# A four-layer graph network kernel: rows of the bf16 pieces of layers one and three padded from 391 to 400 columns

## The chip, the cores and the metric

The kernel runs on one core of one Trainium2 chip. Its time is the device time of one execution in microseconds (us). Lower is better. Three runs of the kernel before gave 3,763.98, 3,763.66 and 3,755.65 us; their median is 3,763.66 us.

## The reference

The input is `x` (3,327 nodes × 512 values, float32) and `adj` (3,327 × 3,327, zero or one). Four layers follow each other. Each first normalises the rows of `x` and takes the positive part (`h`), and adds its result to `x`. Layers one to three are graph attention with 8, 4 and 8 heads, the fourth is an average over neighbours between two dense products:

```python
h = relu(layernorm(x))
Wh = h @ W                                     # per head: 64 columns (128 in the second layer)
e = leaky_relu(f1[:, None] + f2[None, :], 0.2) # f1 = Wh.a1, f2 = Wh.a2, one number a node and head
e = where(adj > 0, e, -9e15)                   # second layer: adj with self loops
x = x + elu(softmax(e, axis=-1) @ Wh)
...
agg = (adj > 0) @ h / max(deg, 1)              # fourth layer
x = x + relu(concat(h @ W_self + b_self, agg @ W_nb + b_nb) @ W_comb + b_comb)
```

## The kernel before, in words

**The algebra.** A leaky ReLU has two slopes, and exp(f1 + f2) is a product. So the weight of neighbour j for node i is one of two products, and which one depends only on the sign of f1(i) + f2(j). The kernel therefore prepares two versions of each node's row: A, scaled by exp(f2), and B, scaled by exp(0.2 f2). Each version has DA = 65 columns a head in layers one and three: 64 of `Wh` and one with the scale itself, whose sum is the softmax's denominator. Each is split into three bf16 pieces, so that their sum has nearly float32's precision: 3 · 65 = 195 columns. For each pair of nodes, a 0-or-2 weight in fp8 says whether A counts (`tht`) or B (`gt`), and attention is then `tht.T @ A + gt.T @ B`.

**Names.** `dims(l)` (L102 to L107) gives the heads H, DA, AO (the column at which B begins in a row: 196 = 195 + one column of ones) and HW (the row's length). In layers one and three (`l` = 0 and 2) the row has 2 · 196 − 1 = 391 columns, A's 195, the one column of ones at 195 that A and B share, and B's 195 from column 196. `abd` (L109 to L116) are these rows in DRAM, a tensor for each group of node tiles. The second layer (`l` = 1) has other rows: A and B apart, 388 columns of bf16 each (L112, L580), or 258 of float32 (L577).

**Tiles.** There are 26 tiles of 128 nodes (the last has 127). As neighbours they go in five groups `JG` of 6, 6, 6, 4 and 4 tiles, as queries in chunks of four (the last has two). `jj` is a tile's place in its group; I call it the row within the group. A tile `ab` holds a group's rows side by side, 6 · 391 columns a partition, row `jj` from column 391 · `jj`.

**A head of a chunk** (`attention`, L505). SP's queue loads `s1b` (L518) and the five groups of `ab` (`load_pieces`, L498 to L503; seven buffers). For each neighbour tile ScalarE (L549) or, for some tiles, VectorE (L546) compares f1 with −f2 into `gt`; two VectorE operations on a whole group combine this with the mask into `tht` and `gt` (L555, L556; seven buffers each). TensorE then runs over the 26 neighbour tiles for two query tiles at a time: for each of the two it loads `tht` as weights and multiplies A's columns (L584), and loads `gt` and multiplies B's (L587), both into one PSUM bank `acc`, A at column 0, B at column AO. So the order is A, B for one query tile, A, B for the next, then the next neighbour tile. In head 0 of layer one alone (`deg`) both products take one column more, the ones, at column 195 (`o` = 1: A ends with it, B begins with it): its sum is the node's degree, copied out by L605. After each pair VectorE adds the three pieces up out of PSUM (L602).

**Work in between.** After each pair `hooks.run` (L471) issues a step of other work: transposing a part of the mask (L187 to L211, layer one), finishing a node tile of this layer (L647) and normalising and projecting it for the next (L397 to L422). That projection writes the pieces: `pieces` (L298) writes ones by a POOL memset (L308), copies two of the pieces by ScalarE (L317, L321), subtracts the third by POOL (L319), and SP stores the tile `pt` to `abd` (L327). For layer one this runs ahead of the attention, in its own stage with two node tiles a store; for layer three it runs inside layer two.

**Order and placement.** The instructions of an engine run in the order that the framework's scheduler gave them from the program's order and from edges that the code adds (`after`, L141). SP's queue issues its DMAs in that order too. Pools of layer `l` lie where an earlier pool lay, and a tile waits for the tiles that lay in its place; `lay_out` (L663) fixes the places, with a `gap` of 20 KB in layer one (L709) that moves `gt` past the stage before it.

Of the kernel before, what the change touches and what calls it, by code (L numbers as in the profile page):

```python
# [25 lines left out]
F32 = mybir.dt.float32  # L26
BF16 = mybir.dt.bfloat16
I32 = mybir.dt.int32
U32 = mybir.dt.uint32
FP8 = mybir.dt.float8e4  # L30
F32R = mybir.dt.float32r
AF = mybir.ActivationFunctionType
ALU = mybir.AluOpType
# [4 lines left out]
P = 128  # L38
# [14 lines left out]
def tile_gnn(ctx: ExitStack, tc: tile.TileContext, x, adj, W0, a01, W1, al, ar, W2, a2,  # L53
# [47 lines left out]

    def dims(l):  # L102

        H = heads[l]
        DA = D // H + 1
        AO = 3 * DA + 1
        return H, DA, AO, (2 * AO - 1 if l != 1 else 2 * AO)  # L107

    abd = []  # L109
    for l in range(3):  # L110
# [187 lines left out]
    def pieces(L, t, AB, pool, first):  # L298

        l = L.l  # L300
        g, jj = jwhere[t]
        H, DA, AO, HW = dims(l)

        o, two = (t % 2, 2) if first else (0, 1)
        if o == 0:
            L.pt = pool.tile([P, H, 2, two, AO] if l == 1 else [P, H, two, HW], BF16, name="pt", bufs=3 if first else 2)
        pt = L.pt
        nc.gpsimd.memset(pt[:, :, :, o, 3 * DA:AO] if l == 1 else pt[:, :, o, 3 * DA:AO], 1.0)  # L308

        def dst(s, a):  # L310
            if l == 1:
                return pt[:, :, a, o, s * DA:(s + 1) * DA]
            return pt[:, :, o, a * AO + s * DA:a * AO + (s + 1) * DA]
        r = pool.tile([P, 2, H, DA], F32, name="r", bufs=2 if first else 1)
        nc.vector.tensor_sub(r, AB, high(AB))  # L315
        for a in range(2):
            nc.scalar.copy(dst(0, a), high(AB[:, a]))  # L317
        for a in range(2):
            nc.gpsimd.tensor_sub(dst(2, a), r[:, a], high(r[:, a]))  # L319
        for a in range(2):  # L320
            nc.scalar.copy(dst(1, a), high(r[:, a]))  # L321
        js = slice(jj + 1 - two, jj + 1)
        if o == two - 1 and l == 1:
            for a in range(2):
                nc.sync.dma_start(abd[l][g][:, a, :, js, :].rearrange("h p j w -> p h j w"), pt[:, :, a])
        elif o == two - 1:
            stored[t] = nc.sync.dma_start(abd[l][g][:, :, js, :].rearrange("h p j w -> p h j w"), pt).ins.name  # L327
# [170 lines left out]
    def load_pieces(L, pool, g, h):  # L498

        nj = JG[g][1]  # L500
        tl = pool.tile([P, JM * 391], BF16, name="ab", bufs=7)
        v = tl[:, :nj * 391].rearrange("p (j w) -> p j w", j=nj)
        return v, nc.sync.dma_start(v, abd[L.l][g][h])  # L503

    def attention(L, hooks, open_next, close):  # L505
# [5 lines left out]
        for c, (t0, nt) in enumerate(chunks):  # L511
# [4 lines left out]
            for h in range(H):  # L516
# [44 lines left out]
                for a in range(2 if l == 1 else 1):  # L561
# [5 lines left out]
                    for ks, js in passes:  # L567
                        thr = {}
                        for j in js:
                            g, jj = jwhere[j]  # L570
                            if l == 1 and KIND[g] != "b" and g not in thr:
                                thr[g] = real(a, g, ks, th)
                            for k in ks:
                                if j == 0:
                                    acc[k] = accs.tile([P, 512], F32, name="acc")
                                if g in thr:
                                    mm = nc.tensor.matmul(acc[k][:, :2 * DA], thr[g][:, k - ks[0], jj, :], ab[a][g][:, jj, :],  # L577
                                                     start=(j == 0), stop=(j == NT - 1), skip_group_check=True)
                                elif l == 1:
                                    mm = nc.tensor.matmul(acc[k][:, :3 * DA], th[a][g][:, k, jj, :], ab[a][g][:, jj, :3 * DA],  # L580
                                                     start=(j == 0), stop=(j == NT - 1), skip_group_check=True)
                                else:
                                    o = 1 if deg else 0
                                    nc.tensor.matmul(acc[k][:, :3 * DA + o], th[0][g][:, k, jj, :],  # L584
                                                     ab[0][g][:, jj, :3 * DA + o], start=(j == 0), stop=False,
                                                     skip_group_check=True)
                                    mm = nc.tensor.matmul(acc[k][:, AO - o:HW], th[1][g][:, k, jj, :],  # L587
                                                     ab[0][g][:, jj, AO - o:HW], start=False, stop=(j == NT - 1),
                                                     skip_group_check=True)
                            if j == JG[3][0]:  # L590
                                late = mm.ins.name
                        if l == 2 and last and h == H - 1:
                            load_y2(yp, 0, late)
                        if js[-1] != NT - 1:
                            continue
                        for k in ks:
                            if l == 1:
                                nc.vector.tensor_reduce(R[:, k, a, :], acc[k][:, :3 * DA].rearrange("p (s d) -> p d s", s=3),
                                                        AX.X, ALU.add)
                            else:  # L600
                                v = acc[k][:, :2 * AO].rearrange("p (a w) -> p a w", a=2)[:, :, :3 * DA]
                                nc.vector.tensor_reduce(R[:, k], v.rearrange("p a (s d) -> p a d s", s=3), AX.X, ALU.add)  # L602
                            if deg:
                                n = pn(t0 + k)
                                nc.vector.tensor_copy(deg2[:n, t0 + k:t0 + k + 1], acc[k][:n, 3 * DA:AO])  # L605
                        gone.append(mm.ins.name)
                        hooks.run(1 if last else 3, hook, 2 if hook % 2 and c == 0 or hook % 3 == 0 and c else 1)
                        hook += 1
# [54 lines left out]
    def lay_out(pool, *tags):  # L663
        for name, n, dt, bufs in tags:
            pool.tile([P, n], dt, name=name, bufs=bufs)
# [8 lines left out]
    lay_out(rp, ("s1b", WMAX, F32, 2))  # L674
    masking = ExitStack()
    bp = masking.enter_context(tc.tile_pool(name="pieces", bufs=1))
    lay_out(bp, ("ab", JM * 391, BF16, 7))
    ip = masking.enter_context(tc.tile_pool(name="masks", bufs=1))
    with tc.tile_pool(name="first", bufs=1) as fp:


        lay_out(fp, ("pt", 16 * 391, BF16, 3), ("AB", 1040, F32, 2), ("r", 1040, F32, 2), ("hT", D, F32, 2))
        xa = []

        def first_x(t, lead=6):
# [15 lines left out]
        while hooks.tiles or hooks.flying:  # L701
# [3 lines left out]
                    ahead[g] = load_pieces(L, bp, g, 0)  # L705
            n += 1
    A, R = ("A", D, F32, 6), ("R", PER * 2 * 129, F32, 1)
    ab, gt, tht = ("ab", JM * 391, BF16, 7), ("gt", PER * JM * P, FP8, 7), ("tht", PER * JM * P, FP8, 7)
    tags = [[A, R, tht, ("gap", 20 * 1024, FP8, 1), gt],  # L709
            [("A", D, F32, 5), ("ab", JM * 258, F32R, 7), R, ("t6", 2 * JM * P, F32R, 4), tht[:3] + (6,), gt[:3] + (6,)],  # L710
            [A, ab, R, tht, gt]]
    hooks.masks = [lambda t=t, g=g: load_mask(ip, t, g) for t in range(NT) for g in range(len(JG))][hooks.done:]
# [532 lines left out]
```

## Time and profile before

| | |
|---|---|
| median of the runs | 3,763.66 us (3,755.65 to 3,763.98) |
| the profiled execution, its own time | 3,765.72 us |
| its span, first to last instruction | 3,763.9 us |
| mean granted TensorE clock | 0.976 of full |
| TensorE busy | 3,548.0 us (94%) |
| VectorE, ScalarE, POOL busy | 2,641.0 (70%), 2,519.9 (67%), 565.1 us (15%) |
| stage before layer one's attention | 0 to about 178 us |
| attention of layer one (L584, L587) | 178 to 1,269 us |
| layer two (L577, L580) | 1,286 to 2,250 us |
| attention of layer three (L584, L587) | 2,279 to 3,404 us |
| fourth layer (L781) | 3,436 to 3,748 us |
| DMA | 773 MB, mean 205 GB/s |
| `ab` loads of layers one and three | 336 of 586.5 KB, 224 of 391.0 KB |
| `pt` stores of layers one and three | 13 of 1,564 KB, 26 of 782 KB |

In the profile PE is TensorE's matmuls, PEld its weight loads, DVE is VectorE, ACT ScalarE, POOL GpSimd, SP the engine whose queue issues most DMAs. Ln is line n of the kernel. Matmuls overlap in the pipe, so their durations add up to more than the time that passed; the distance from one start to the next tells the pace. A wait is put down to what ended it last, and idle time of an engine that others don't wait for costs nothing.

### The profile page before, as it was taken

What the parts mean: (1) busy time and instruction counts of PE and PEld (TensorE: products, weight loads), DVE (VectorE), ACT (ScalarE), POOL (GpSimd) and SP (SyncE); (2) the same over time, 40 slices, a digit from 0 to 9 for tenths busy, and PEclk for the clock granted to TensorE, in tenths of its full rate; (3) what the DMA queues carried; (4) which work ended last, traced back from release to release, by engine and by line L of the source; (5) the groups of instructions that cost most, each with busy time, mean ns of one, the idle gap of its engine ahead of it and who ended that gap; (6) DMA issues with size and microseconds to landing.
All of it is one profiled execution on the core that took longest, in us unless ns stands there. A gap on an engine that the chain in (4) does not pass through costs nothing. (4 is left out here: it accounts for less than half of the span.)

```text
span 3763.9 us, 78861 instructions
## 1 busy us (share of the span) xinstructions
PE 3548.0 (94%) x31348; PEld 3198.3 (85%) x31348; DVE 2641.0 (70%) x5230; ACT 2519.9 (67%) x4170; POOL 565.1 (15%) x832
## 2 busy tenths in 40 slices
PE   7799999999999888999999978999999999999998
PEld 5699999999999677887887867999898989886886
DVE  7688888888777677878778766776766767672221
ACT  5677887778788667777768766776766767572111
POOL 6502221202101101122122121010000101010000
PEclk9899999999999999999999999999999999999999
DMA  7777767777657767767767786555555545576431
GB/s 216 225 207 212 218 203 220 224 219 223 206 191 247 247 226 246 237 220 251 251 215 243 250 282 200 185 180 163 188 169 167 192 159 194 163 259 237 129 102 50
DMA packets 321403, 773.06 MB, mean 205 GB/s; under 512 B 36037, under 2 KB 143560, under 8 KB 320384
## 3 DMA queue, kind: packets, MB, share of 16 engines
q1 hardware_dynamic: 293920, 707.23, 57.6%
q0 software_dynamic: 27104, 60.69, 6.6%
q8 instruction: 249, 4.08, 0.4%
q14 instruction: 130, 1.06, 0.1%
HBM read 661.25 MB, written 128.68 MB: 210 GB/s over the span
## 5 line engine op out<-in xcount | busy, mean ns | idle before, releaser
L549 ACT ACTIVATE gt<-s1b,ks 128x512 fp8e4<-128x512 f32 (+1 forms) x2968 | 1759.9, 678 | 291.1 <-issue 150.4
L584 PE MATMUL acc<-ab,tht 128*128 128x195 bf16 (+1 forms) x10816 | 1875.6, 248 | 20.5 <-DVE tht L555 15.0
L587 PE MATMUL acc<-ab,gt 128*128 128x195 bf16 (+1 forms) x10816 | 1874.9, 249 | 3.9 <-DVE gt L556 3.1
L584 PEld LDWEIGHTS <-tht 128*128 128x128 fp8e4 x10816 | 1061.0, 98 | 27.2 <-DVE tht L555 16.1
L587 PEld LDWEIGHTS <-gt 128*128 128x128 fp8e4 x10816 | 1053.7, 97 | 28.3 <-issue 16.1
L555 DVE TENSOR_TENSOR tht<-gt,m 128x768 uint32<-128x768 uint32 (+3 forms) x700 | 557.5, 798 | 184.7 <-ACT gt L549 179.7
L577 PE MATMUL acc<-ab,t 128*128 128x258 f32 x4160 | 576.4, 298 | 72.8 <-DVE t L493 62.5
L577 PEld LDWEIGHTS acc<-ab,t 128*128 128x128 f32 x4160 | 543.9, 200 | 100.8 <-DVE t L493 76.6
L556 DVE TENSOR_TENSOR gt<-tht,m 128x768 uint32<-128x768 uint32 (+3 forms) x700 | 563.4, 806 | 8.5
L546 DVE TENSOR_SCALAR gt<-s1b,ns 128x512 fp8e4<-128x512 f32 (+1 forms) x672 | 318.3, 485 | 142.0 <-PE acc L587 140.0
L781 PE MATMUL acc<-y,mf 128*128 128x512 f32 x1352 | 309.8, 391 | 1.3 <-DVE mf L776 1.3
L657 POOL TENSOR_TENSOR xt<-xt,e 128x512 f32<-128x512 f32 x78 | 113.1, 1450 | 1273.3 <-DVE e L656 1228.6
L781 PEld LDWEIGHTS acc<-y,mf 128*128 128x128 f32 x1352 | 253.5, 188 | 57.4 <-DVE mf L776 1.8
L602 DVE TENSOR_REDUCE R<-acc 128x130 f32<-128x390 f32 x416 | 214.8, 556 | 82.9 <-PE acc L587 82.8
L778 ACT CAST mf<-m 128x768 fp32r<-128x768 fp8e4 (+1 forms) x78 | 59.1, 762 | 244.7 <-PE acc L781 232.9
L493 ACT CAST t<-gt 128x1536 fp32r<-128x1536 fp8e4 x104 | 150.6, 1473 | 101.8 <-PE acc L577 101.6
L340 PE MATMUL mm<-w,hT 128*128 128x260 f32 (+1 forms) x832 | 200.2, 393 | 17.3 <-ACT hT L138 11.4
L319 POOL TENSOR_TENSOR pt<-r 128x520 bf16<-128x520 f32 (+1 forms) x116 | 139.2, 1219 | 369.2 <-DVE r L315 304.2
L340 PEld LDWEIGHTS mm<-w,hT 128*128 128x128 f32 x832 | 157.3, 194 | 42.4 <-ACT hT L138 14.0
L377 PE MATMUL mm<-w,hT 128*128 128x512 f32 x352 | 159.3, 596 | 0.0
L493 ACT CAST t<-tht 128x1536 fp32r<-128x1536 fp8e4 x104 | 149.7, 1462 | 9.0 <-DVE tht L555 5.7
L289 ACT ACTIVATE h<-xt,mv 128x512 f32<-128x512 f32 x104 | 84.2, 811 | 101.9 <-POOL mv L287 101.9
(132 smaller groups left out, 2893.1 us busy)
## 6 DMA issues: line engine op xcount, KB each, us to landing
ab<-ab SPq DMA_DIRECT2D x336, 586.5 KB
ab<-ab SPq DMA_DIRECT2D x224, 391.0 KB
ab<-ab SPq DMA_DIRECT2D x112, 774.0 KB
ab<-ab SPq DMA_DIRECT2D x112, 516.0 KB
ab<-ab SPq DMA_DIRECT2D x56, 582.0 KB
s1b<-s SPq DMA_DIRECT2D x120, 256.0 KB
m<-mask SPq DMA_DIRECT2D x72, 384.0 KB
ab<-pt SPq DMA_DIRECT2D x40, 516.0 KB
```

What stands on the lines that cost most here:

```text
L340: nc.tensor.matmul(pw, hT[:, k, :], L.w[:, k, f, :], start=(k == 0), stop=(k == KC - 1))
L377: nc.tensor.matmul(pw, hT[:, k, :], L.w[i][:, k, :], start=(k == 0), stop=(k == KC - 1))
L493: (nc.scalar.copy if KIND[g] == "s" else nc.vector.tensor_copy)(t[:, :k1 - k0, :nj], th[a][g][:, k0:k1])
L546: nc.vector.tensor_scalar(gv[:, :, jj, :], s1v, L.ns2[:, j, h:h + 1], 2.0, op0=ALU.is_gt, op1=ALU.mult, saturate=False)
L549: nc.scalar.activation(gv[:, :, jj, :], s1v, AF.Relu, bias=L.ks2[:, j, h:h + 1], scale=BIG, saturate=False)
L555: nc.vector.tensor_tensor(pu, gu, mu, ALU.bitwise_and)
L556: nc.vector.tensor_tensor(gu, pu, mu, ALU.bitwise_xor)
L577: mm = nc.tensor.matmul(acc[k][:, :2 * DA], thr[g][:, k - ks[0], jj, :], ab[a][g][:, jj, :], start=(j == 0), stop=(j == NT - 1), skip_grou ...
L584: nc.tensor.matmul(acc[k][:, :3 * DA + o], th[0][g][:, k, jj, :], ab[0][g][:, jj, :3 * DA + o], start=(j == 0), stop=False, skip_group_che ...
L587: mm = nc.tensor.matmul(acc[k][:, AO - o:HW], th[1][g][:, k, jj, :], ab[0][g][:, jj, AO - o:HW], start=False, stop=(j == NT - 1), skip_gro ...
L602: nc.vector.tensor_reduce(R[:, k], v.rearrange("p a (s d) -> p a d s", s=3), AX.X, ALU.add)
L781: nc.tensor.matmul(acc[k], mf[:, jj, :], y2[g][:, jj, s, :], start=(j0 + jj == 0 and s == 0), stop=(j0 + jj == NT - 1 and s == 1))
```

## The change

Rows of layers one and three get 400 columns in place of 391, 800 bytes in place of 782. AO, the column at which B begins, becomes 200, so B begins 400 bytes after A and each row 800 bytes after the one before. A and B now have a column of ones each, at 195 and 395, and four more columns that no product reads (196 to 199, 396 to 399). The memset fills five columns of both halves. The matmuls take the same number of columns as before: 195, or 196 in head 0 of layer one; B's go to columns 200 and up of `acc`. The degree is now the sum of two columns of `acc`, 195 and 395. Tiles, DRAM tensors, loads and stores grow with the row, and the gap in layer one's placement shrinks from 20 to 19 KB. The second and fourth layers compute as before.

```diff
@@ -101,10 +101,11 @@
 
     def dims(l):
 
+
         H = heads[l]
         DA = D // H + 1
-        AO = 3 * DA + 1
-        return H, DA, AO, (2 * AO - 1 if l != 1 else 2 * AO)
+        AO = -(-(3 * DA + 1) // 8) * 8 if l != 1 else 3 * DA + 1
+        return H, DA, AO, 2 * AO
 
     abd = []
     for l in range(3):
@@ -305,7 +306,8 @@
         if o == 0:
             L.pt = pool.tile([P, H, 2, two, AO] if l == 1 else [P, H, two, HW], BF16, name="pt", bufs=3 if first else 2)
         pt = L.pt
-        nc.gpsimd.memset(pt[:, :, :, o, 3 * DA:AO] if l == 1 else pt[:, :, o, 3 * DA:AO], 1.0)
+        nc.gpsimd.memset(pt[:, :, :, o, 3 * DA:AO] if l == 1 else
+                         pt[:, :, o].rearrange("p h (a w) -> p h a w", a=2)[..., 3 * DA:AO], 1.0)
 
         def dst(s, a):
             if l == 1:
@@ -498,8 +500,9 @@
     def load_pieces(L, pool, g, h):
 
         nj = JG[g][1]
-        tl = pool.tile([P, JM * 391], BF16, name="ab", bufs=7)
-        v = tl[:, :nj * 391].rearrange("p (j w) -> p j w", j=nj)
+        HW = dims(L.l)[3]
+        tl = pool.tile([P, JM * HW], BF16, name="ab", bufs=7)
+        v = tl[:, :nj * HW].rearrange("p (j w) -> p j w", j=nj)
         return v, nc.sync.dma_start(v, abd[L.l][g][h])
 
     def attention(L, hooks, open_next, close):
@@ -584,8 +587,8 @@
                                     nc.tensor.matmul(acc[k][:, :3 * DA + o], th[0][g][:, k, jj, :],
                                                      ab[0][g][:, jj, :3 * DA + o], start=(j == 0), stop=False,
                                                      skip_group_check=True)
-                                    mm = nc.tensor.matmul(acc[k][:, AO - o:HW], th[1][g][:, k, jj, :],
-                                                     ab[0][g][:, jj, AO - o:HW], start=False, stop=(j == NT - 1),
+                                    mm = nc.tensor.matmul(acc[k][:, AO:AO + 3 * DA + o], th[1][g][:, k, jj, :],
+                                                     ab[0][g][:, jj, AO:AO + 3 * DA + o], start=False, stop=(j == NT - 1),
                                                      skip_group_check=True)
                             if j == JG[3][0]:
                                 late = mm.ins.name
@@ -602,7 +605,8 @@
                                 nc.vector.tensor_reduce(R[:, k], v.rearrange("p a (s d) -> p a d s", s=3), AX.X, ALU.add)
                             if deg:
                                 n = pn(t0 + k)
-                                nc.vector.tensor_copy(deg2[:n, t0 + k:t0 + k + 1], acc[k][:n, 3 * DA:AO])
+                                nc.vector.tensor_reduce(deg2[:n, t0 + k:t0 + k + 1],
+                                                        acc[k][:n, 3 * DA:AO + 3 * DA + 1:AO], AX.X, ALU.add)
                         gone.append(mm.ins.name)
                         hooks.run(1 if last else 3, hook, 2 if hook % 2 and c == 0 or hook % 3 == 0 and c else 1)
                         hook += 1
@@ -674,12 +678,12 @@
     lay_out(rp, ("s1b", WMAX, F32, 2))
     masking = ExitStack()
     bp = masking.enter_context(tc.tile_pool(name="pieces", bufs=1))
-    lay_out(bp, ("ab", JM * 391, BF16, 7))
+    lay_out(bp, ("ab", JM * 400, BF16, 7))
     ip = masking.enter_context(tc.tile_pool(name="masks", bufs=1))
     with tc.tile_pool(name="first", bufs=1) as fp:
 
 
-        lay_out(fp, ("pt", 16 * 391, BF16, 3), ("AB", 1040, F32, 2), ("r", 1040, F32, 2), ("hT", D, F32, 2))
+        lay_out(fp, ("pt", 16 * 400, BF16, 3), ("AB", 1040, F32, 2), ("r", 1040, F32, 2), ("hT", D, F32, 2))
         xa = []
 
         def first_x(t, lead=6):
@@ -705,8 +709,8 @@
                     ahead[g] = load_pieces(L, bp, g, 0)
             n += 1
     A, R = ("A", D, F32, 6), ("R", PER * 2 * 129, F32, 1)
-    ab, gt, tht = ("ab", JM * 391, BF16, 7), ("gt", PER * JM * P, FP8, 7), ("tht", PER * JM * P, FP8, 7)
-    tags = [[A, R, tht, ("gap", 20 * 1024, FP8, 1), gt],
+    ab, gt, tht = ("ab", JM * 400, BF16, 7), ("gt", PER * JM * P, FP8, 7), ("tht", PER * JM * P, FP8, 7)
+    tags = [[A, R, tht, ("gap", 19 * 1024, FP8, 1), gt],
             [("A", D, F32, 5), ("ab", JM * 258, F32R, 7), R, ("t6", 2 * JM * P, F32R, 4), tht[:3] + (6,), gt[:3] + (6,)],
             [A, ab, R, tht, gt]]
     hooks.masks = [lambda t=t, g=g: load_mask(ip, t, g) for t in range(NT) for g in range(len(JG))][hooks.done:]
```

## The prediction

> **What bounds the kernel now.** I read the page's shares and slices first, then the cost groups, then a table of stretches, and last the timeline of the matrix engine inside one head. From the page (engine, busy us, share, instructions; then tenths of busy time in 40 slices; then line, engine, op, count | busy us, mean ns of one | idle before, releaser):
>
> ```profile
> span 3763.9 us, 78861 instructions
> PE 3548.0 (94%) x31348; PEld 3198.3 (85%) x31348; DVE 2641.0 (70%) x5230; ACT 2519.9 (67%) x4170; POOL 565.1 (15%) x832
> ...
> PE   7799999999999888999999978999999999999998
> ...
> L584 PE MATMUL acc<-ab,tht 128*128 128x195 bf16 (+1 forms) x10816 | 1875.6, 248 | 20.5 <-DVE tht L555 15.0
> L587 PE MATMUL acc<-ab,gt 128*128 128x195 bf16 (+1 forms) x10816 | 1874.9, 249 | 3.9 <-DVE gt L556 3.1
> ```
>
> L584 and L587 are the first and third layers' matmuls, 21,632 of the 31,348, and hardly ever wait. The stretches (us, busy us of each engine, granted clock, DMA share, GB/s) say that both layers run at the matrix engine's pace; the first row is layer one's attention, the second layer three's:
>
> ```profile
> 175.00:1270.00 1095.00, 1069.54 (x11895) 1049.65 (x11895) 899.58 (x1830) 853.67 (x1515) 164.80 (x252) 0.99 0.73 219
> 2280.00:3404.00 1124.00, 1119.10 (x11339) 1014.38 (x11338) 800.10 (x1612) 765.12 (x1307) 91.60 (x131) 1.00 0.55 184
> ```
>
> The mean of 248 ns is useless here: matmuls overlap. What counts is the time from one start to the next. The timeline (start, length) of rows 4 and 5 of a group of six, layer three:
>
> ```profile
> 2622.30 0.25 PE L584 MATMUL acc<-ab,tht 128*128 128x195 bf16 x1
> 2622.38 0.24 PE L587 MATMUL acc<-ab,gt 128*128 128x195 bf16 x1
> 2622.47 0.25 PE L584 MATMUL acc<-ab,tht 128*128 128x195 bf16 x1
> 2622.55 0.25 PE L587 MATMUL acc<-ab,gt 128*128 128x195 bf16 x1
> 2622.63 0.25 PE L584 MATMUL acc<-ab,tht 128*128 128x195 bf16 x1
> 2622.72 0.25 PE L587 MATMUL acc<-ab,gt 128*128 128x195 bf16 x1
> 2622.81 0.25 PE L584 MATMUL acc<-ab,tht 128*128 128x195 bf16 x1
> 2622.89 0.25 PE L587 MATMUL acc<-ab,gt 128*128 128x195 bf16 x1
> ```
>
> The page rounds to 10 ns; the same records in ns give steps of 88, 83, 84, 83 (row 4), then 88, 87, 83, 88 (row 5). So there is a fast matmul and a slow one. I sorted all steps of both layers (chunks after the first, heads after the first in layer one) by row within the group and by order: A then B for one query tile, A then B for the next. A starts 782·row bytes into the tile, B 392 bytes later. Means in ns, stalls of 95 ns and more left out:
>
> ```
> row  A at mod 16  B at mod 16   A     B     A     B
> 0        0            8        83.9  88.0  83.3  86.9
> 1       14            6        86.7  86.9  83.4  87.8
> 2       12            4        86.7  87.0  83.4  87.0
> 3       10            2        86.7  83.3  84.8  84.5
> 4        8            0        88.4  83.3  83.3  83.4
> 5        6           14        88.3  86.7  83.3  87.7
> ```
>
> The two operands that start on 16 bytes (A of row 0, B of row 4) are at or near 83.3; most others are 3 to 5 ns slower, though a misaligned A is slow only the first time. The middle layer gives a second witness: L580's rows are 776 bytes, so rows 0 to 5 start at 0, 8, 0, 8, 0, 8 modulo 16. Its 387-column matmuls, first of each pair, take 163.4 to 164 ns in rows 2 and 4 and 168.3 in rows 1, 3 and 5 (row 0, which often follows another kind of matmul, 164 or 174). Row 2 starts at 16 modulo 32, where the new B will lie, and is fast.
>
> **What the skill says.** "SBUF — State Buffer", Specifications (TRN2): lines are of 16 bytes and each cross to a new line pays a penalty; it gives no price for a matmul's start. The trace agrees on the 16 and prices it at about 5 ns. "TensorE: Matmul & The Clock Gate", "Wait — 56ns, not 53.3ns?": warm matmuls start N ÷ 2.4 GHz + about 2.5 ns apart, 83.8 ns for 195 columns (estimate); the trace has 83.3 for aligned ones and 56 for the 128-column transposes of L202. So 83.3 is the floor, and 83.4 with rounding is what I use. "DMA: Bandwidth & Descriptors", "How a descriptor splits into AXI transactions": a row that does not start at 256 bytes costs extra beats. The trace shows no such price: median packets of 4,096, 4,692 and 6,192 bytes took 160, 181 and 236 ns, all 25.6 to 26.2 bytes per ns.
>
> **The change, part by part.**
>
> 1. *Aligned operands.* Rows become 800 bytes and B starts 400 after A: everything is at 0 or 16 modulo 32. Layer one has 10,589 unstalled steps of mean 85.72 ns, layer three 10,736 of 85.63. Excess over 83.4: 10,589 × 2.32 = 24.5 us and 10,736 × 2.23 = 23.9 us, 48.4 in all. In layer three PE is busy 1,119 of 1,124 us, VectorE 71% and ScalarE 68%, so nearly all of it comes through: 23.5. In layer one VectorE is at 82%, ScalarE at 78% and PE already idles 25 us, so a little is lost to later feeders: I take 22 (bounds 12 and 24.5). Sum −45.5. If the matrix engine speeds up, the next thing late would be `tht` (L555 on VectorE), which waits for ScalarE's `gt` (L549); both idle mostly for PE to free buffers. Column counts, matmul count and weight loads stay; B moves from column 196 to 200 of its PSUM bank, from one even column to another, and I give that nothing.
>
> 2. *Bytes.* Loads grow 400/391: 586.5 KB to 600.0, 391.0 to 400.0. Loads and stores together 333 MB to 341 (packets of 4,692, 3,128, 1,564 and 782 bytes). One load packet goes from 181 to some 185 ns. DMA shares of 0.73 and 0.55 become about 0.75 and 0.57 (and rise another 2% as the layers shorten); seven buffers for five loads per head keep them hidden: PE waited 5.4 us for `ab` in the whole run. Without that cover each load of 600 KB costs about 0.06 us more. SP issues the same number in the same order. Nothing here.
>
> 3. *Stage before attention (0 to 175 us).* Stores of `pt` grow 1,564 to 1,600 KB; POOL waited 24.6 us here for such stores to free `pt`, and 13 × 36 KB at 218 GB/s is 2.1 us at most. The POOL memset (L308) writes 80 elements a tile in place of 8. Now 134 ns median; no row shows 80. Bounds: no more at all, or the subtraction's rate (L319, 1,182 ns for 520, 2.3 ns each), 72 × 2.3 = 0.16 us, 26 times 4.3 us. PE waits for none of it directly, but POOL is busy 114 of 175 us and its mean/variance steps (L285 to L287) queue behind. I take +1 for stores and memsets together, bounds 0 and 6. The 26 memsets for layer three lie inside the middle layer, where POOL is mostly idle.
>
> 4. *Degree.* 26 one-column copies (L605, 148 ns) become two-element reduces on VectorE. No row shows one; between 148 ns and the 556 ns of L602, so at most 26 × 0.4 = 10 us of VectorE in head 0 alone, while PE's 208 matmuls run 17.8 us per head. Behind it are the reduction of the next tile and the hooks. Nothing taken; 2 us at worst, for PE.
>
> 5. *Placement.* Tiles move by some hundred bytes; in layer one the gap shrinks by 1,024 bytes, so the first `gt` comes to lie over the end of the second `hT` instead of `xt`. It then waits for tile 25's projection (L340 ended 168.7 us) but is first written on ScalarE at 173.5: hidden by 4.8 us. The scheduler could order something differently; I allow ±4 us for that, half the spread of the three runs.
>
> Sum: 3,763.9 − 45.5 + 1 = 3,719.4 us of span. The profiled execution took 3,765.7, 1.8 more than its span: 3,721.2. It lies 2.1 above the median of the runs shown: **3,719**.
>
> **Rivals.**
>
> *Feeders take half of layer one's gain.* For: PE's 25 us of idle time there; VectorE 82%. Against: its wait for `gt` (80 us here) lies behind ScalarE, and ScalarE waits 57 us for PE to give buffers back. 3,719 + 10 to 12 = 3,730; 3,741 if layer one gains nothing.
>
> *B at 16 modulo 32 stays slow.* B would be 87.3 in every row, against a mean of 86.2 now, A 83.4 against 85.1: 10,816 × (1.7 − 1.1) = 6 us, 3,758. Against: L580's row 2. For: head 0 of layer one, whose B starts at the odd column 195 in tile and bank (390 bytes after A): all its B steps take 86.6 to 88.6 ns, row 3 too, where B lies at 16 modulo 32 (86.6 and 87.5). An odd start in the bank explains that as well, and I think it the likelier cause since only there are all six rows slow.
>
> *It isn't alignment* but the weights' address or the order of A and B. For: a misaligned A is fast on second use. Then nothing changes but bytes: 3,763 to 3,767.
>
> *Slower: padded loads become the bound of layer one.* All DMA there takes 0.73 × 1,095 = 799 us, of which `ab` packets are 436 (half of 590.6 + 280.7, sums over 16 engines), the rest 363. They bind from 436·x + 363 > 1,073, so from x = 1.63 times the present packet time. At x = 2 layer one takes 1,235 us, layer three stays hidden: 3,764 + 140 − 23 = 3,881. Against: packet time goes with bytes, and x should be 1.02.
>
> **How the numbers follow.** Forecast 0.71 (own range 3,711 to 3,728), half lost 0.14, B slow 0.07, not alignment 0.03, slower 0.05. Within 0.3% (11.3 us, about what a measurement can tell) are the B-slow and not-alignment cases. Faster 0.85, same 0.10, slower 0.05. The range runs from the full excess with a favourable order (3,708) to layer one without gain (3,741).
>
> **What would show it.** Right: steps of L584 and L587 have one value near 83.4 in all rows and both layers; layer three's stretch shortens by about 23 us, layer one's by about 22, the middle and last stages by nothing; `ab` packets take some 185 ns. Wrong: B steps at 87 (line of 32 bytes); steps at 83 but longer waits of L584 on `tht` or `ab` (feeders, loads); the start of L584 later than 178 us by more than a few us (memset, stores, placement).

## The result, and the profile after

The changed kernel took 3,732.6 us (median; 3,726.8 to 3,739.0) against 3,760.8 (3,755.7 to 3,764.0) for the kernel before: a ratio of 0.9927, interval 0.9915 to 0.9939, so 28 us less. The forecast was 3,719, 45 us less than the median that it started from (3,763.7). The sign and the place were right and the size was not: somewhat under two thirds of the gain came.

The page of the kernel after, the same rows as were shown of before. Its lines are two or three numbers further on: L587 and L590 here are L584 and L587 of before.

```profile
span 3736.9 us, 78857 instructions
PE 3524.4 (94%) x31348; PEld 3172.3 (85%) x31348; DVE 2638.8 (71%) x5230; ACT 2519.9 (67%) x4170; POOL 558.9 (15%) x832
...
PE   7799999999999888999989988999999999998998
...
L587 PE MATMUL acc<-ab,tht 128*128 128x195 bf16 (+1 forms) x10816 | 1847.4, 248 | 20.9 <-DVE tht L558 13.8
L590 PE MATMUL acc<-ab,gt 128*128 128x195 bf16 (+1 forms) x10816 | 1846.4, 248 | 12.0 <-ACT gt L552 7.2
```

The two matmul groups lost 28 us each of modelled busy time; they overlap, so this isn't 56 us. The idle time ahead of L590 grew from 3.9 to 12.0 us. Its stretches, layer one and layer three (us, busy us of each engine, granted clock, DMA share, GB/s):

```profile
172.00:1256.00 1084.00, 1056.12 (x11893) 1034.58 (x11894) 896.75 (x1826) 850.54 (x1510) 163.12 (x249) 0.99 0.74 223
2262.00:3376.00 1114.00, 1107.75 (x11355) 1001.30 (x11356) 800.48 (x1616) 768.15 (x1315) 90.86 (x132) 1.00 0.56 189
```

These windows are laid around the layers in whole microseconds. Layer three's is 1,114 us long in place of 1,124, with PE still busy for all but 6 of them. Layer one's is 1,084 in place of 1,095, and PE is idle for 28 us of it, where it was for 25. From the first to the last start of the two lines, the profiled executions split like this (us):

| stretch | before | after | difference | predicted |
|---|---|---|---|---|
| up to layer one's attention | 177.7 | 172.1 | −5.6 | +1 |
| layer one's attention | 1,091.0 | 1,083.9 | −7.1 | −22 |
| between | 1,009.8 | 1,006.6 | −3.2 | 0 |
| layer three's attention | 1,125.7 | 1,113.4 | −12.3 | −23.5 |
| rest | 359.7 | 360.8 | +1.1 | 0 |

A second profile of the changed kernel has 173.7, 1,080.5, 1,000.9, 1,113.0 and 360.3. The middle part differs by 6 us between these two executions, so its −3.2 alone shows nothing; all profiles together say a little more (below, at the stage before attention).

Now the matmuls. To escape the 10-ns rounding I compare starts that lie 48 matmuls apart, at one place: layer three, third chunk, head 3, neighbour tiles 6 to 18. The timeline of the kernel before (start, length; the 47 lines between are left out), then of the kernel after:

```profile
2682.15 0.25 PE L584 MATMUL acc<-ab,tht 128*128 128x195 bf16 x1
...
2686.26 0.25 PE L584 MATMUL acc<-ab,tht 128*128 128x195 bf16 x1
```

```profile
2662.43 0.25 PE L587 MATMUL acc<-ab,tht 128*128 128x195 bf16 x1
...
2666.47 0.25 PE L587 MATMUL acc<-ab,tht 128*128 128x195 bf16 x1
```

4.11 us became 4.04; in ns 4,108 and 4,040, so 85.6 and 84.17 a step. Over whole layers the unstalled steps fell from 85.72 to 84.17 ns in layer one and from 85.63 to 84.17 in layer three, and they are the same in every row of a group, for A and for B, and in head 0. That is the uniform step that was forecast, but at 84.17 and not at 83.4: (85.72 − 84.17) × 10,589 = 16.4 us and (85.63 − 84.17) × 10,736 = 15.7 us, 32 in place of 48.

What layer one then lost again is in the waits of PE (engine, line waited for: us in all, times, longest). Before, in layer one's attention (lines of other matmuls left out):

```profile
PE acc L584 <- DVE tht L555: 14.5, 4, 8.5
...
PE acc L584 <- DMA ab<-ab: 4.1, 3, 1.9
...
PE acc L587 <- DVE gt L556: 1.8, 3, 0.6
PE acc L587 <- ACT gt L549: 0.4, 1, 0.4
```

After:

```profile
PE acc L587 <- DVE tht L558: 11.0, 4, 8.5
PE acc L590 <- ACT gt L552: 6.1, 2, 5.7
PE acc L587 <- DMA ab<-ab: 5.0, 3, 2.5
...
PE acc L590 <- DVE gt L559: 1.7, 4, 0.6
PE acc L590 <- DVE rc L620: 1.5, 3, 0.8
```

The waits of these two lines rose from 21 to some 25 us. The new 5.7-us wait on ScalarE's `gt` is in head 2 of the first chunk, where before stood one of 4.3 us on `tht`: in both kernels VectorE runs a long series of other work there (L272 and L273 of before) between the steps that feed PE. A wider measure takes in the pace after a wait too: all steps of 95 ns or more between neighbouring matmuls of the two lines, each less 84.2 ns. These slow steps of layer one add up to 22.3 us before, 30.5 after and 27.2 in the second profile; in layer three 3.7, 6.4 and 6.2. So of 16.4 us that the matmuls save in layer one, 5 to 8 go back to late feeders and to the slow stretches behind waits (last section); of 15.7 in layer three, 2.6.

### The profile page after: what moved, and what is told of

Read it like the earlier page. It is cut to its first block, busy times and chain, and to the rows that moved or that the text cites. A ratio compares the mean times of both kernels' runs of the same rounds, so it can differ in the third digit from the quotient of the medians.

```text
span 3736.9 us, 78857 instructions
## 1 busy us (share of the span) xinstructions
PE 3524.4 (94%) x31348; PEld 3172.3 (85%) x31348; DVE 2638.8 (71%) x5230; ACT 2519.9 (67%) x4170; POOL 558.9 (15%) x832
## 3 DMA queue, kind: packets, MB, share of 16 engines
q8 instruction: 249, 4.08, 0.4%
## 5 line engine op out<-in xcount | busy, mean ns | idle before, releaser
L587 PE MATMUL acc<-ab,tht 128*128 128x195 bf16 (+1 forms) x10816 | 1847.4, 248 | 20.9 <-DVE tht L558 13.8
L590 PE MATMUL acc<-ab,gt 128*128 128x195 bf16 (+1 forms) x10816 | 1846.4, 248 | 12.0 <-ACT gt L552 7.2
L590 PEld LDWEIGHTS <-gt 128*128 128x128 fp8e4 x10816 | 1061.5, 98 | 40.0 <-issue 18.8
L587 PEld LDWEIGHTS <-tht 128*128 128x128 fp8e4 x10816 | 1061.9, 98 | 27.5 <-DVE tht L558 15.4
L580 PE MATMUL acc<-ab,t 128*128 128x258 f32 x4160 | 579.9, 299 | 73.8 <-DVE t L495 62.7
L580 PEld LDWEIGHTS acc<-ab,t 128*128 128x128 f32 x4160 | 548.1, 202 | 101.5 <-DVE t L495 76.3
L559 DVE TENSOR_TENSOR gt<-tht,m 128x768 uint32<-128x768 uint32 (+3 forms) x700 | 563.9, 806 | 8.5
L290 ACT ACTIVATE h<-xt,mv 128x512 f32<-128x512 f32 x104 | 84.2, 810 | 100.9 <-POOL mv L288 96.9
```

The costliest lines, as they stand in the source:

```text
L559: nc.vector.tensor_tensor(gu, pu, mu, ALU.bitwise_xor)
L590: mm = nc.tensor.matmul(acc[k][:, AO:AO + 3 * DA + o], th[1][g][:, k, jj, :], ab[0][g][:, jj, AO:AO + 3 * DA + o], start=False, stop=(j == ...
```

## The experiments

Two explanations stood at the start. **Start on 16 bytes**: an operand is fast when it begins at a multiple of 16 bytes, which is what the change says. **B at 16 modulo 32**: something of B is still slow, so that a lower floor would be had at 32 bytes. A third came up after the first of these runs. **Same offset and fewest lines**: what counts is how many lines of 16 bytes an operand covers (a line begins at each multiple of 16 bytes) and whether consecutive operands begin at one offset within a line. The later runs split the third. Beside these stood two rivals: that the gain came from another order of the work or from the loads, and that weight loads set the pace. Every diff is against the kernel after; "..." stands for lines left out, among them those that only fit tile sizes to the edit. "Steps" are the mean unstalled times from one start to the next in layer one and in layer three, in ns.

**The change again**, on the chip of the next three:

> The changed kernel once more, as the base for the others of this call. Every theory: 3,725 to 3,740 us, steps from one matmul's start to the next 84.17 ns in all rows and in both layers. If the stage ahead of layer one's attention (177.7 us before, 172.1 in the changed kernel's first trace) is shorter because of the change, it ends near 172 us again; if that was chance, it scatters between 172 and 178.

3,731.2 us, ratio 0.9922 [0.9905, 0.9939] to a median of 3,761.6; steps 84.17 and 84.17.

**Everything 8 bytes further.** The tile gets 8 more columns and the view begins at column 4, so that A and B of every row start at 8 modulo 16:

```diff
-        tl = pool.tile([P, JM * HW], BF16, name="ab", bufs=7)
-        v = tl[:, :nj * HW].rearrange("p (j w) -> p j w", j=nj)
+        tl = pool.tile([P, JM * HW + 8], BF16, name="ab", bufs=7)
+        v = tl[:, 4:nj * HW + 4].rearrange("p (j w) -> p j w", j=nj)
...
```

> The changed kernel with every operand A and B moved 8 bytes on in its buffer (8 or 24 modulo 32 in place of 0 or 16); bytes, loads, columns and results as in the changed kernel. Theory that the start on 16 bytes is what helps: steps go back to a mean of 85.5 to 88 ns, 30 to 80 us more PE time in the two layers, total 3,755 to 3,800 us. Rival that the gain came from another order of the work or from the loads: steps stay at 84.2 and the time at that of the changed kernel.

3,729.0 us, 0.9913 [0.9896, 0.9929], steps 84.17 in both layers. The timeline at the same place:

```profile
2654.08 0.25 PE L587 MATMUL acc<-ab,tht 128*128 128x195 bf16 x1
...
2658.12 0.25 PE L587 MATMUL acc<-ab,tht 128*128 128x195 bf16 x1
```

4.04 us, as with offset 0. No operand of this kernel begins on 16 bytes, and nothing is lost: the first explanation, which the prediction shared, fell. A gain from another order or from the loads would look just like this; that rival falls only with the shifts by 14 and 12 bytes below, which keep the rows, the sizes of the loads and the padding and lose the gain.

**Layer three on 32 bytes.** Half-rows of 208 columns (416 bytes) there:

```diff
-        AO = -(-(3 * DA + 1) // 8) * 8 if l != 1 else 3 * DA + 1
+        AO = -(-(3 * DA + 1) // (8 + 4 * l)) * (8 + 4 * l) if l != 1 else 3 * DA + 1
...
```

> The changed kernel with rows of 416 columns in layer three alone, so that there A and B both begin at a multiple of 32 bytes. Theory that the start at 16 modulo 32 keeps B (and through it all steps) at 84.17 in place of 83.4: layer three's steps fall to 83.3 to 83.4, its stretch by 9 us, layer one stays. Rival that 84.17 is the floor for 195 columns (columns taken in pairs[...]): layer three stays at 84.17, the time within 4 us of the changed kernel. Rival that weight loads set the pace: likewise 84.17.

3,737.2 us, 0.9929 [0.9913, 0.9946], layer three's steps 84.16. The second explanation fell too: 84.17 isn't a B that is still slow. The time is 6 us above the change, where 4 were allowed; the intervals overlap, and in the profile layer three takes 1,113.7 us, as with the change.

**One column less.** Except for j = 0 and head 0 of layer one, both matmuls take 194 columns. The column left out is the third bf16 piece of the softmax denominator, so that this kernel leaves out a part of it:

```diff
+                                    e = 0 if deg or j == 0 else 1
-                                                     ab[0][g][:, jj, :3 * DA + o], start=(j == 0), stop=False,
+                                                     ab[0][g][:, jj, :3 * DA + o - e], start=(j == 0), stop=False,
...
-                                                     ab[0][g][:, jj, AO:AO + 3 * DA + o], start=False, stop=(j == NT - 1),
+                                                     ab[0][g][:, jj, AO:AO + 3 * DA + o - e], start=False, stop=(j == NT - 1),
```

> The changed kernel with 194 in place of 195 columns in the matmuls of layers one and three, except for the first neighbour tile of each sum and for head 0 of layer one: what is left out is the third bf16 piece of the softmax denominator (worth about 2 to the -17 of it). Theory that columns are taken in pairs: steps fall from 84.17 to 83.33 ns, 0.83 x about 20,000 matmuls, 16 us less of PE time, total 10 to 17 us below the changed kernel. Theory that the pace is proportional to single columns: 83.75, 8 us less. Rival that weight loads set the pace: 84.17, no change.

3,718.2 us, 0.9883 [0.9866, 0.9899], 13 us less than the change. Steps 83.47 and 83.36; at the same place:

```profile
2650.11 0.25 PE L588 MATMUL acc<-ab,tht 128*128 128x194 bf16 x1
...
2654.11 0.25 PE L588 MATMUL acc<-ab,tht 128*128 128x194 bf16 x1
```

4.00 us, 83.33 a step. One column less is worth 0.83 ns, while 195 and 196 columns (head 0) both take 84.2: columns seem to count in pairs, as far as these three counts tell. That the weight loads set the pace is refuted: they are the same here. So 84.17 is the lowest pace that any kernel here kept up with 195 columns, and the 83.4 of the prediction is that of 194.

**Offsets 14, 12 and 2.** The edit of the 8-byte shift with 7, 6 and 1 for the 4:

> The changed kernel with every operand moved 14 bytes on: all begin at 14 modulo 16, an odd column, and spread over 26 lines of 16 bytes in place of 25. New theory (after the 8-byte shift cost nothing): what costs is that one operand lies at another offset modulo 16 than the one before it, not the offset itself; then steps stay at 84.17. Rival that a line takes a fixed time (26 lines of 3.33 ns): steps of 86.67, 50 us more. Rival that an odd column is what costs: steps of 85 to 88.

> The changed kernel with every operand moved 12 bytes on: an even column, but 26 lines of 16 bytes. Theory that each line takes 3.33 ns (26 lines 86.67, and 25 lines less than the 84.17 that 195 columns take): 86.7 everywhere, 55 us of PE time more than the changed kernel, total 3,765 to 3,775. Rival that the 14-byte shift was slow for its odd column: 84.17 and the changed kernel's time.

> The changed kernel with every operand moved 2 bytes on: an odd column in 25 lines. Line theory: 84.17 everywhere, 3,727 to 3,738 us. Rival of the odd column: 85 to 88, 20 to 80 us more.

One execution of each: 3,771.1, 3,773.9 and 3,745.0 us (before: 3,759.5 beside the first, 3,761.4 beside the others). Steps 86.71, 86.70 and 84.99; the means of the rows lie within 0.5 ns of each other. The timelines at the usual place, of 12 and then of 2 bytes:

```profile
2683.24 0.25 PE L587 MATMUL acc<-ab,tht 128*128 128x195 bf16 x1
...
2687.40 0.25 PE L587 MATMUL acc<-ab,tht 128*128 128x195 bf16 x1
```

```profile
2662.04 0.25 PE L587 MATMUL acc<-ab,tht 128*128 128x195 bf16 x1
...
2666.12 0.25 PE L587 MATMUL acc<-ab,tht 128*128 128x195 bf16 x1
```

4.16 and 4.08 us. An operand has 390 bytes. From offsets 0, 2 and 8 it covers 25 lines of 16 bytes (at most 398 bytes), from 12 and 14 it covers 26 (402 and 404). The two slow kernels share the 26 lines, not an odd column: 12 is an even one and as slow as 14. 86.7 is 26 × 3.33, the figure that was expected of lines; since no kernel here covers 27, that each further line costs 3.33 is not shown. With 25 lines an odd start (2 bytes) costs 0.83 ns over an even one: of the two expectations for it, that of the lines (84.17) missed, and that of the odd column (85 to 88, 20 us or more) held at its lower edge in the steps and came with some 13 us in the time. The kernels with 12 and 14 took some 12 us more than the kernel before, although every row is padded: it isn't the padding that helps, but the offset that it gives.

**A at 0, B at 8.** Half-rows of 196 columns, so that A starts at 0 and B at 8 modulo 16 in every row; both offsets are fast alone. The tiles are 392 columns wide and the gap is 20 KB again:

```diff
-        AO = -(-(3 * DA + 1) // 8) * 8 if l != 1 else 3 * DA + 1
+        AO = -(-(3 * DA + 1) // 4) * 4 if l != 1 else 3 * DA + 1
...
```

> The changed kernel with rows of 392 columns and B at column 196: every A at 0 modulo 16, every B at 8, so the offset changes with each matmul, but all columns are even and rows are multiples of 16 bytes. Theory of the changing offset: a mean of 85 to 86.5 ns, with slow steps of 86 to 88 every second time, most of the gain lost (20 us or more). Rival that only odd columns or a 26th line cost: 84.17 everywhere, and the time of the changed kernel.

3,747.3 us in one execution (before 3,759.5). Steps 85.08 in the mean, and they alternate: 83.3 from an A to its B, 86.8 from a B to the next A. The timeline at the usual place:

```profile
2666.57 0.25 PE L587 MATMUL acc<-ab,tht 128*128 128x195 bf16 x1
...
2670.66 0.24 PE L587 MATMUL acc<-ab,tht 128*128 128x195 bf16 x1
```

Some 4.08 us for the 48. So a change of offset between 0 and 8 from one operand to the next costs 0.9 ns in the mean. In time some 16 us of the gain are lost, less than the 20 that were expected. And this kernel shows the trap: 83.3 ns is a step that no kernel here kept up with 195 columns; it comes only in turn with 86.8. I take it that the fast one makes up for part of the slow one before it. How, no run shows, but neither of the two is a floor.

**A and B alike, rows of 399.** B 400 bytes after A, rows 798 bytes apart: A and B of a row share an offset, which goes 0, 14, 12, 10, 8, 6 through the group as A's did before. The columns of ones need two memsets:

```diff
-        return H, DA, AO, 2 * AO
+        return H, DA, AO, 2 * AO - (l != 1)
...
+        nc.gpsimd.memset(pt[:, :, :, o, 3 * DA:AO] if l == 1 else pt[:, :, o, 3 * DA:AO], 1.0)
+        if l != 1: nc.gpsimd.memset(pt[:, :, o, AO + 3 * DA:HW], 1.0)
...
```

> The changed kernel with rows of 399 columns and B still at column 200: A and B of one row share the offset modulo 16 (0, 14, 12, 10, 8, 6 in rows 0 to 5), which changes from row to row alone. Theory of the changing offset: one slow step in four (a row's first A or the last B before it), a mean between 84.4 and 85.4. Rival that the offset itself costs, odd rows or a 26th line: all four steps of rows 1 and 2 (26 lines) or of rows 1, 3 and 5 (odd columns) slow, the others 84.17.

3,770.2 us in one execution; steps 85.55 and 85.50. By row: 0 and 4 near 84.3, 3 and 5 near 85.0 and 84.8, 1 and 2 at 86.7 to 87.0. In the mean of its four steps each row takes the time of its own offset. Row 3 also tells the line from the offset: at 10 modulo 16 it takes 84.97 ns with 195 columns, which fit in 25 lines, and 86.8 in head 0 of layer one, where 196 columns (392 bytes) reach into a 26th. Weighted (rows 0 to 3 five of 26 each, rows 4 and 5 three each), the shifts' values, with that of 2 bytes for 6 and 10, give 85.40, so that the change of offset between rows, which is every fourth step, adds only 0.1 in the mean. The steps are a little shorter than in the kernel before and the time is some 10 us longer. In the profiles the attentions of the two layers are no longer than before (1,090.4 and 1,125.7 us), while the stage ahead takes 180.3 us (before 177.7) and the middle 1,012.2 (1,009.8).

**B's sums at an odd column of the bank.** B's matmuls write to column 197 in place of 200:

```diff
-                                    mm = nc.tensor.matmul(acc[k][:, AO:AO + 3 * DA + o], th[1][g][:, k, jj, :],
+                                    mm = nc.tensor.matmul(acc[k][:, AO - 3:AO - 3 + 3 * DA + o], th[1][g][:, k, jj, :],
...
```

> The changed kernel with B's sums at column 197 of the PSUM bank (an odd column) in place of 200; what is read stays as it is. Head 0 of layer one had every B step slow before (86.6 to 88.6 ns), where B began at the odd column 195 in tile and bank. Theory that the odd start in the bank did that: B's steps become 86 to 88. Rival that it was the offset of what is read, which moved on by 390 bytes from A: steps stay at 84.17.

3,732.4 us in one execution; steps 84.22 and 84.17. With 195 columns an odd column in the bank costs nothing. With the 196 of head 0 it costs a little: there the steps from A to B take 85.0 ns and those from B to A 84.2, where both take 84.2 in the changed kernel. Neither comes near the 86.6 to 88.6 of head 0 before, which the prediction put down to the bank. What is left for those is where the operands lie in the tile; which of its effects it was, no run separates.

**One layer each.** Only the first, then only the third layer padded; the other keeps rows of 391 columns with its tiles and its memset:

```diff
-        AO = -(-(3 * DA + 1) // 8) * 8 if l != 1 else 3 * DA + 1
-        return H, DA, AO, 2 * AO
+        AO = -(-(3 * DA + 1) // 8) * 8 if l == 0 else 3 * DA + 1
+        return H, DA, AO, 2 * AO - (l == 2)
...
```

> The change made in layer one alone, layer three with its rows of 391 columns. From the steps: layer one at 84.17, layer three at 85.63; 10,589 x 1.55 = 16.4 us less, some of it lost to stalls, and some 4 us from a shorter stage ahead if that belongs to layer one's even rows: 3,741 to 3,750 us. If layer one gives nothing in the end (stalls take it): 3,757 to 3,764.

> The change made in layer three alone, layer one with its rows of 391 columns and the stage ahead as before. From the steps: layer three at 84.17, 10,736 x 1.46 = 15.7 us less, hardly any of it lost: 3,744 to 3,751 us. Layer one at 85.7, first matmul of its attention near 177 us; at 172 to 175 if the shorter stage is chance or comes from elsewhere.

First only: 3,747.8 us, 0.9967 [0.9954, 0.9979]. Third only: 3,741.6, 0.9954 [0.9937, 0.9970]; before 3,761.4. The gains are 13.7 and 19.9, in sum 33.5 against 28 to 30 for both together: within the intervals. Third only came out some 2 us below the range expected. The timeline of the first-only kernel, the usual place in layer one and then in layer three:

```profile
561.33 0.25 PE L587 MATMUL acc<-ab,tht 128*128 128x195 bf16 x1
...
565.37 0.25 PE L587 MATMUL acc<-ab,tht 128*128 128x195 bf16 x1
...
2660.11 0.25 PE L587 MATMUL acc<-ab,tht 128*128 128x195 bf16 x1
...
2664.22 0.25 PE L587 MATMUL acc<-ab,tht 128*128 128x195 bf16 x1
```

4.04 us in the padded layer, 4.11 in the other. Third only:

```profile
569.01 0.25 PE L587 MATMUL acc<-ab,tht 128*128 128x195 bf16 x1
...
573.12 0.25 PE L587 MATMUL acc<-ab,tht 128*128 128x195 bf16 x1
...
2662.36 0.25 PE L587 MATMUL acc<-ab,tht 128*128 128x195 bf16 x1
...
2666.39 0.25 PE L587 MATMUL acc<-ab,tht 128*128 128x195 bf16 x1
```

The other way round. Each layer's steps depend on its own rows alone. The slow steps of layer one follow too: 26.6 us where its rows are padded, 19.6 where they aren't. In all six profiles with steps of 84.16 to 84.22 in layer one they add up to 24.3 to 30.5 us, in the two with rows of 391 columns to 19.6 and 22.3.

**All of it on one scale.** The matmuls' steps in ns, where nothing stalls:

| columns | offset of A, B (mod 16) | lines of 16 bytes | step |
|---|---|---|---|
| 194 | 0, 0 | 25 | 83.3 |
| 195 | 0, 0 or 8, 8 | 25 | 84.17 |
| 195 | 2, 2 | 25 | 85.0 |
| 195 | 0, 8 | 25 | 85.08 |
| 195 | 12, 12 or 14, 14 | 26 | 86.7 |

This accounts for most of the kernel before. Its A's lie at 0, 14, 12, 10, 8, 6: with 84.17, 86.7, 86.7, 85.0, 84.17, 85.0, weighted as above, 85.40. Its B's lie at 8, 6, 4, 2, 0, 14: 84.78. (Here 6 and 10 are taken to cost what 2 costs, which the rows of 399 bear out, and 4 what 0 costs, which no run tried.) Mean 85.09, against 85.65 measured. So by this sum, of the 1.48 ns that a step fell, 0.92 (62%) come from operands with 26 lines or an odd start, and 0.56 are left for offsets that change from A to B, for which the kernel with 0 and 8 showed 0.9. That lines and starts cost this much is shown by the shifts. How the reads and the matmuls' order make the remaining 0.56, no run here settles.

## Why the prediction was right or wrong

**1, aligned operands.** Right that the matmuls' bytes in the tile set their pace, that both layers would become uniform, and that nothing but the layout is needed. Two terms of the sum failed. The first is the floor of 83.4 ns: it was read off the fast one of two modes, and no kernel here kept those fast steps up without slow ones between them. The sustained floor is 84.17, so that 0.77 ns × 21,325 steps = 16 us of the 48.4 were never there. The estimate from the Trainium skill ("TensorE: Matmul & The Clock Gate", "Wait — 56ns, not 53.3ns?"), 83.8 ns, was nearer than the prediction's reading of the trace; for 194 and 195 columns the runs show 83.3 and 84.17.

The second is how much of layer one comes through: 22 of 24.5 was taken, 7 to 11 of 16.4 came. PE's wait on the feeders was named as what would be late next, `tht` and `gt`, and they were late, by 5 to 8 us. Layer three, where PE is hardly ever idle, let 12.3 of 15.7 through, not all. Of the 32 us that the steps save, 19 and 23 thus came off the two layers in the two profiles, 60 to 72%. Two other kernels give somewhat more, set against the changed one: with 194 columns the steps save 0.70 × 10,585 + 0.81 × 10,719 = 16 us against the change and the time fell by 13; with 12 bytes they cost 2.53 × 21,300 = 54 us and the time rose by 41. There some 80% of what PE gains or loses reaches the end.

Luck made the miss look smaller. In the profiled executions the two layers got 19.4 us shorter, where 45.5 were forecast, a miss of 26; the rest of the kernel got 7.7 us shorter, where 1 us more was forecast. So over a quarter of the 27 us between the two spans did not come from where the gain was expected.

The reason given was also too narrow. "Start on 16 bytes" isn't the condition: 8 bytes do as well, 12 and 14 are worse than the mixture before, and equal offsets matter besides. The forecast held since padding to 16 bytes meets all of the conditions at once. "SBUF — State Buffer", Specifications (TRN2), which names lines of 16 bytes and a penalty for crossing into a new one, fits the 26th line, which costs 2.5 ns a matmul (86.7 against 84.17); what the crossings into the 25 lines before it cost does not show.

The second witness of the prediction, the middle layer's L580, spoke against that reason. Both matmuls of a pair there read the very same columns. In rows 1, 3 and 5, at 8 modulo 16, the first takes 168 ns and the second 163.4 (rows 1 and 3; behind row 5 another kind of matmul follows): what is slow is not the place, but the first matmul after the offset went from 0 to 8. From 8 back to 0 (rows 2 and 4) nothing is slow, as in the kernel with A at 0 and B at 8.

**2, bytes.** As forecast. Packets of 4,800 bytes took 185 ns in the median, and the DMA share rose from 0.73 to 0.74 in layer one and from 0.55 to 0.56 in layer three. PE's waits for `ab` there were 4.1 and 5.0 us. The slower rival, loads that bind, didn't show.

**3, the stage before attention.** The memset is what was bounded; from the groups of the kernel after (count: least, median, most ns, first to last):

```profile
L309 POOL MEMSET pt<- x58: 128/172/457, 0.9 to 2241.7; 128x80 bf16 x52, 128x8 bf16 x6
```

172 ns where before had 134: 26 × 0.04 = 1 us on POOL. But the stage ended 5.6 us earlier, not 1 later. In the eleven profiles with rows of `pt` of 800 or 784 bytes in layer one, attention starts at 170.3 to 175.1 us; in the three with 782 or 798 it starts at 175.4 (third only), 177.7 (before) and 180.3 (rows of 399), so the two groups just don't overlap. POOL's waits for stores of `pt` up to 180 us (us in all, times, longest), before and after:

```profile
POOL pt L308 <- DMA ab<-pt: 24.6, 10, 11.0
```

```profile
POOL pt L309 <- DMA ab<-pt: 16.2, 6, 7.6
```

They are 15.0 to 18.4 us in those eleven and 22.3 to 26.2 in those three. The stores' packets themselves take 72 to 78 ns in the mean in all of these. That rows of whole 16 bytes let the stores finish sooner is thus likely and not shown; no run here changes these stores alone.

Layer three's stores, which run in the middle part, point the same way, and so does that part's −3.2 us. Packets of 782 or 798 bytes took 49 to 56 ns in the mean there, packets of 784, 800 or 832 bytes 42 to 44. The middle part took 1,006.7 to 1,012.2 us in the three profiles with the former and 1,000.4 to 1,006.6 in the ten with 800 or 832 bytes; but with 784 bytes it took 1,009.0, so this too is not shown.

**4, degree.** As forecast at nothing: the reduce takes hardly longer than the copy did (150 ns against 148).

```profile
L608 DVE TENSOR_REDUCE deg<-acc x26: 144/150/153, 193.3 to 1171.3; 128x1 f32<-128x2 f32 x25, 127x1 f32<-127x2 f32 x1
```

**5, placement.** The order of the instructions did change, on PE and on the engines that feed it; what it cost or gave was not separated from the rest.

**The rivals.** "Feeders take half of layer one's gain" came nearest in time (3,730), in part by luck, since it counts on the floor of 83.4 as well; that 5 to 8 of 16.4 us were lost again bears it out in part. "B at 16 modulo 32" and "not alignment" are refuted by the uniform 84.17, by the layer on 32 bytes and by the shifts. The measured time lies 5 us above the forecast's own range, 3,711 to 3,728; the floor alone is worth 16.

## What to carry to other kernels

Lay out moving operands so that they cover the fewest 16-byte lines, begin at an even bf16 column, and all at the same offset; that is what these operands of 194 to 196 bf16 columns show. And count columns in pairs, since dropping an odd one was worth 13 us here, if the result can do without it. Take a floor from a long sum of steps, never from the fast mode of a mixture, for a fast step may only come in turn with a slow one. Where another engine is at 80%, count on only part of what the bound engine gains: here about half in that layer.

## What the runs showed of the hardware

From one matmul's start to the next it takes 83.3 ns with 194 columns, 84.17 with 195 and 85.0 with 195 from an odd start, 0.83 ns apart each time; with 26 lines of 16 bytes it takes 86.7, which is 3.33 ns a line.

A wait of some 2 us can cost more than its length. In layer one of the kernel after, third chunk, head 3, PE waits 2.0 us for a transfer, until 562.5 us. It then runs at 84 ns a step for 1.4 us, and goes on like this from 563.9 us:

```profile
565.23 0.37 PE L587 MATMUL acc<-ab,tht 128*128 128x195 bf16 x1
565.40 0.37 PE L590 MATMUL acc<-ab,gt 128*128 128x195 bf16 x1
565.56 0.37 PE L587 MATMUL acc<-ab,tht 128*128 128x195 bf16 x1
...
567.42 0.25 PE L587 MATMUL acc<-ab,tht 128*128 128x195 bf16 x1
567.51 0.25 PE L590 MATMUL acc<-ab,gt 128*128 128x195 bf16 x1
```

Steps of 164 ns, some 21 of them, and then 84 again from 567.3 us: 1.7 us on top of the wait. The granted clock of this stretch is 0.50 in the trace, and 1.00 before and after it. The Trainium skill, "TensorE: Matmul & The Clock Gate", "Part 1: The HAM clock gate (the "warmup" mystery)", describes a clock that halves after an idle window of about 3.4 us. Here the engine need not have been idle for as long: in the 3.4 us before the clock fell PE had been busy for 1.4 us. All fourteen profiles agree. Leaving out the first 8 us of each attention, the clock falls 40 times in the two layers, each time for 3.4 or 6.8 us, and PE had never been busy for more than 1.62 of the 3.4 us before. Single shorter waits passed without it: at 399 us two starts lie 1.4 us apart, and no slow step follows. Steps of 150 to 200 ns, nearly all of this kind, make up 8.2 us of layer one's 22.3 us of slow steps before, and 10.2 of 30.5 after. So a feeder that is late can be paid for twice.
